# A two-layer decoder on one core: queries and keys of the causal attentions laid out by DMA through DRAM instead of by padded products, and a new rank for the order of work

## The chip, the cores and the metric

The kernel runs on one core of a Trainium2 chip. The metric is the device time of one execution in microseconds. Three runs of the kernel before gave 4504.14 (the median), 4497.92 and 4506.57 us.

## What is computed

Sixteen sequences of 512 rows and 256 features pass through two decoder layers. Each layer is a causal self-attention, a cross-attention to 64 context rows, and a feed-forward part, each added to its input and normalised. All data are 32-bit floats. Only the two causal attentions are touched by the change. Cut to what matters:

```python
# layer 0: 16 heads of 16 features, a bias that depends on (i - j)
q, k, v = split(x @ Wqkv.T)                       # heads() splits 256 into 16 x 16
logits = q @ k.T / 4 + fourier_bias(alpha, beta)[h, i - j]
x = layernorm(x + softmax(causal(logits)) @ v @ Wout.T)
x = layernorm(x + cross_attention_0(x, ctx))      # 16 heads
x = layernorm(x + experts(x))                     # 8 routed (top 2) and 2 shared
# layer 1: q, k, v through latents of 64 features, no bias
q, k, v = x @ wq_lat @ wq_heads, x @ wk_lat @ wk_heads, x @ wv_lat @ wv_heads
x = layernorm(x + softmax(causal(q @ k.T / 4)) @ v @ w_proj + b_proj)
x = layernorm(x + cross_attention_1(x, ctx))      # one head
x = layernorm(x + feed_forward(x))                # 1024 hidden, sine, relu
```

The bias of layer 0 is a sum of cosines and sines of (i - j). With the angle-sum formulas it becomes 16 more features beside the 16 of each head: fixed cosines and sines on the query side, the same mixed by alpha and beta on the key side.

## The kernel before

**Layout of an attention.** A group is four heads, and there are four groups. A tile q or k of a group is 128 x 512: head j has partitions 32 j to 32 j + 31, of which the first 16 hold its features and the other 16 the extra ones. Score products then contract over 32 partitions, and four heads run on four row bands of TensorE's array at once. In layer 1 the extra rows are zeros, but for row 16: there k holds -1 and q later receives the row's maximum, so that the product subtracts it.

**How q and k come about** (`queries_keys`, lines 825 and 869). The weight matrices are padded on the host (`_laid_out`): each head's 16 columns stand in 32, the others are zero. So every group needs products of its own with 128 output rows, half of them padding. In layer 0 a group takes two products of 512 columns for q, two for k and one more (`kmat` by `qfeat`) for k's bias features; VectorE evicts q and adds `qfeat`, ScalarE evicts k. In layer 1 a group takes one product of 64 contracted rows for q, and one on the array's other 64 rows for k; ScalarE evicts both, k with the bias `onerow`. The results are the tiles q and k themselves, with no transfer in between.

**The attention** (`causal_attention`, line 557). The scores are made twice: once with queries as rows (`max_unit`), reduced by VectorE to row maxima, and once with keys as rows (`exp_unit`), from which the maximum is subtracted within the product (layer 0: the product `mrow` by `minus16`; layer 1: by q's extra row) and which ScalarE exponentiates, GpSimd masks and a product with the values (`po`) consumes. Units of a group's maxima run beside units of the exponentials of the group before. q and k have three buffers each.

**The order of work.** The stages of a sequence are a0 (attention of layer 0), d0 (cross-attention 0 and experts), a1 and d1 (cross-attention 1 and feed-forward). `places` (line 1402) pairs a1 of one sequence with d0 of the next, and d1 with a0 of the one after. All operations are recorded first, each with an engine, an estimated cost and an estimated time until its result can be used. `run_plan` (line 346) then lists them: at each step it takes, among the operations that can start soonest, the one with the lowest rank. The rank is set in `stage` (line 318): the stage's place plus the share of the stage's TensorE cost that is recorded before the operation, less 0.5 for operations that use one of the pools named in `score_pools`. The instructions are issued in that order, and `Pinned` (line 330) keeps every engine's own order as planned. TensorE, VectorE, ScalarE and GpSimd are pinned so; DMAs on SyncE's queue (SP), x, context, mask and the output, are not. Every engine's queue is in order: a waiting instruction holds up all behind it on that engine.

**Buffers.** Pool `d4` (six of 4 KB per partition) serves the d stages: transposed input, queries, score tiles e, results. Pool `h` (three) serves the experts' hidden rows. Three PSUM banks `pd` take all products but scores and attention values.

Of the kernel before, what the change touches and what calls it, by code (L numbers as in the profile page):

```python
# [26 lines left out]
F32 = mybir.dt.float32  # L27
# [3 lines left out]
ALU = mybir.AluOpType  # L31
# [28 lines left out]
def decoder_kernel(ctx: ExitStack, tc: tile.TileContext, a: dict, out: bass.AP):  # L60
# [34 lines left out]

    wqk0 = weight("wqk0", 2 * NG * P)
    qfeat = const.tile([P, S], F32, tag="qfeat", name="qfeat")
    load(qfeat, a["qfeat"])
    kmat = const.tile([P, NG * P], F32, tag="kmat", name="kmat")
    load(kmat, a["kalpha"])  # L100
    with tc.tile_pool(name="once", bufs=1) as once:
        for name, op in (("kbeta", ALU.add), ("kbeta_n", ALU.subtract)):
            part = once.tile([P, NG * P], F32, tag="part", name=name)
            load(part, a[name])
            nc.vector.tensor_tensor(kmat, kmat, part, op)
    wv0 = weight("wv0", D)
    wout0 = weight("wout0", D)
# [21 lines left out]
    nc.gpsimd.memset(minus16, -1.0)  # L129
    onerow = const.tile([P, 1], F32, tag="onerow", name="onerow")  # L130
    load(onerow, a["onerow"])

# [35 lines left out]
    for n, name in enumerate(("wq_lat", "wk_lat", "wv_lat")):  # L168
        load(wlat[:, :, n], a[f"L1_attn_{name}"].rearrange("(c p) n -> p c n", p=P))
    wqk1 = const.tile([P, NG * P], F32, tag="wqk1", name="wqk1")  # L170
    load(wqk1, a["wqk1"])
# [93 lines left out]
    e_pool, os_pool = Pool("e", 4), Pool("os", 1)  # L265
    d4, h_pool, u_pool = Pool("d4", 6), Pool("h", 3), Pool("u", 1)
    ctx_pool, mi_pool, cT_pool, vbd_pool = Pool("ctx", 1), Pool("mi", 4), Pool("cT", 3), Pool("vbd", 2)
# [47 lines left out]

    score_pools = ("pa", "e", "q", "k", "os", "mrow", "m", "r", "a4")

    def stage(place, record, *args):

        stage_ops.clear()  # L320
        record(*args)
        done, total = 0.0, sum(o.cost for o in stage_ops if o.engine == "PE") or 1.0
        for o in stage_ops:

            ahead = 0.5 if any(s.pool.name in score_pools for s in o.slots) else 0.0
            o.rank = place + done / total - ahead
            if o.engine == "PE":
                done += o.cost
# [14 lines left out]

    pe, dve, act, pool = map(Pinned, (nc.tensor, nc.vector, nc.scalar, nc.gpsimd))

# [211 lines left out]
    def causal_attention(queries_keys, exact):  # L557
# [6 lines left out]
        def max_unit(g, w, pair):  # L564
# [33 lines left out]

            return first, None, masks, follow, [q, k], [two]

        def exp_unit(g, w, pair):
# [41 lines left out]

            return first, None if exact else second, None, follow, [q, k] + ([] if exact else [groups[g]["mrow"]]), [two]

# [15 lines left out]
        def rows_of_maxima(g):  # L661
            q, wide, token = groups[g]["q"], *((whole, "whole") if exact else (parts, "parts"))
            p = ps_d([P, 512], "pr", F32 if exact else BF16)

            def turn():
                for i in range(NT):
                    pe.transpose(
                        p.t[:, i * P : (i + 1) * P],
                        wide[:, i].rearrange("p j r -> p (j r)"),
                        ident if exact else ident16,  # L670
                    )

            PE(0.45 if exact else 0.25, turn, [token], [p])
            if exact:
                DVE(S, lambda: dve.tensor_tensor(q.t, p.t, q.t, ALU.add), [p, q], [q])
            else:
                mrow = groups[g]["mrow"] = mrow_pool([P, S], "mrow", BF16)
                ACT(S, lambda: act.copy(mrow.t, p.t), [p], [mrow])
# [64 lines left out]
        while last is None or n <= last:  # L743
# [5 lines left out]

            while len(groups) < NG and (n_m + 2) // 6 >= len(groups):  # L750
                g = len(groups)
                q, k = queries_keys(g)
                groups[g] = dict(q=q, k=k, m=small([P, NT, NG, 1], "m"))
            for g in [g for g, r in rows_at.items() if r == n]:
# [53 lines left out]
    def fill_values(t, p):  # L808

        ACT(D, lambda: act.copy(vp[:, t, :, :HD], p.t[:, :D].rearrange("p (h d) -> p h d", d=HD)), [p], [("vp", t)])  # L810

    def attention0(x):
        xT = features(x, a4)
# [10 lines left out]

        def queries_keys(g):
            q, k = q_pool([P, S], "q"), k_pool([P, S], "k")
            p = ps_d([P, 512], "pq")
            PE(
                mm_cost(S, 2),
                lambda: mm_chunks(p.t, lambda c: wqk0[:, c, g * P : (g + 1) * P], lambda c: xT.t[:, c]),  # L830
                both(xT), [p],
            )
            DVE(S, lambda: dve.scalar_tensor_tensor(q.t, p.t, HD**-0.5, qfeat, ALU.mult, ALU.add), [p], [q])
            p2 = ps_d([P, 512], "pk")

            def keys():
                for c in range(NC):
                    pe.matmul(
                        p2.t, wqk0[:, c, (NG + g) * P : (NG + g + 1) * P], xT.t[:, c], start=(c == 0), stop=False
                    )  # L840
                pe.matmul(p2.t, kmat[:, g * P : (g + 1) * P], qfeat, start=False, stop=True)

            PE(mm_cost(S, 3), keys, both(xT), [p2])
            ACT(S, lambda: act.copy(k.t, p2.t), [p2], [k])
            return q, k

        yT = causal_attention(queries_keys, False)
        project_norm(x, yT, wout0)

    def attention1(x):  # L850
# [17 lines left out]

        def queries_keys(g):
            q, k = q_pool([P, S], "q"), k_pool([P, S], "k")  # L870
            p, p2 = ps_d([P, 512], "pq"), ps_d([P, 512], "pk")
            cols = slice(g * P, (g + 1) * P)
            PE(
                mm_cost(S),
                lambda: pe.matmul(p.t, wqk1[0:64, cols], lat.t[0:64, 0], start=True, stop=True), [lat[0]], [p],
            )
            ACT(S, lambda: act.mul(q.t, p.t, HD**-0.5), [p], [q])
            PE(
                mm_cost(S),
                lambda: pe.matmul(p2.t, wqk1[64:128, cols], lat.t[64:128, 0], start=True, stop=True), [lat[0]], [p2],  # L880
            )
            ACT(S, lambda: act.activation(k.t, p2.t, AF.Identity, bias=onerow), [p2], [k])
            return q, k

        for t in range(NT):
# [8 lines left out]
            fill_values(t, pv)  # L894
        yT = causal_attention(queries_keys, True)
        project_norm(x, yT, wproj)
# [469 lines left out]
    def inputs(b):  # L1366
        x, c, mi = x_pool([P, NT, D], "x"), ctx_pool([SK, D], "ctx"), mi_pool([P, SK], "mi", I32)
        op(
            "SP", 0.1, lambda: nc.sync.dma_start(x.t, a["x"][b].rearrange("(t p) d -> p t d", p=P)),
            (), rows_of(x), wait=6.0,  # L1370
        )

        def small_ones():
            nc.sync.dma_start(c.t, a["ctx_1024"][b])
            nc.sync.dma_start(mi.t, a["mask_BxS2_ik0"][b].partition_broadcast(P))

        op("SP", 0.1, small_ones, (), [c, mi], wait=4.0)
        seqs[b] = [x, c, mi]
# [14 lines left out]
    def d1(b):  # L1393
# [3 lines left out]
        op(  # L1397
            "SP", 0.1, lambda: nc.sync.dma_start(out[b].rearrange("(t p) d -> p t d", p=P), x.t),
            rows_of(x), (), wait=5.0,
# [18 lines left out]
def _laid_out(i):  # L1418
# [6 lines left out]
    wqkv = np.asarray(i["L0_attn_Wqkv"]).T  # L1425
    qk = z((D, 2, H, 32), np.float32)
    qk[:, :, :, :HD] = wqkv[:, : 2 * D].reshape(D, 2, H, HD)
    a["wqk0"] = qk.reshape(D, -1)
    a["wv0"] = wqkv[:, 2 * D :]
    a["wout0"] = np.asarray(i["L0_attn_Wout"]).T  # L1430
    heads = z((2, 64, H, 32), np.float32)
    heads[0, :, :, :HD] = np.asarray(i["L1_attn_wq_heads"]).reshape(64, H, HD)
    heads[1, :, :, :HD] = np.asarray(i["L1_attn_wk_heads"]).reshape(64, H, HD)
    a["wqk1"] = heads.reshape(P, -1)

    R = HD // 2
    omega = 10000.0 ** (-2.0 * np.arange(R) / HD)
    angle = omega[:, None] * np.arange(S)[None, :]
    trig = z((4, 32, S), np.float32)
    trig[:, 16:24], trig[:, 24:32] = np.cos(angle), np.sin(angle)  # L1440
    a["qfeat"] = trig.reshape(P, S)
    alpha, beta = np.asarray(i["L0_attn_alpha"]), np.asarray(i["L0_attn_beta"])
    ka, kb, kn = (z((P, H, 32), np.float32) for _ in range(3))
    for r in range(R):
        cos, sin = 16 + r, 24 + r
        ka[cos, :, cos] = ka[sin, :, sin] = alpha[:, r]
        kb[cos, :, sin] = kn[sin, :, cos] = beta[:, r]
    a["kalpha"], a["kbeta"], a["kbeta_n"] = (k.reshape(P, -1) for k in (ka, kb, kn))
    p = np.arange(P)
    a["hmask"] = (p[:, None] // HD == np.arange(H // NC)[None, :]).astype(np.float32)  # L1450
    a["vmask"] = (p[:, None] // SK == np.arange(2 * HD)[None, :] // HD).astype(np.float32)
    a["onerow"] = -(p % 32 == HD).astype(np.float32)[:, None]
    a["prio"] = np.tile(np.arange(NE, 0, -1, dtype=np.float32), (P, 1))
# [18 lines left out]
```

## Time and profile before

| | us |
|---|---|
| median of three runs | 4504.14 |
| the profiled execution, its time | 4507.05 |
| its span, first to last instruction | 4505.3 |
| TensorE's matmuls, busy (PE) | 4260.3 |
| VectorE, busy (DVE) | 2641.7 |
| ScalarE, busy (ACT) | 1571.0 |
| GpSimd, busy (POOL) | 1205.5 |
| first instruction of TensorE, which waits for the first context | 50.0 |

In the profile PE is TensorE's matmuls and PEld its weight loads. A row of a timeline gives the start, the duration, the engine, the line of the code that issued it (all work of the plan has the line of one helper), the operation, out <- in by the program's names and a count of records; a bracket gives the idle time of the engine before it and what ended it. The profile counts two records for one product of 32-bit floats. Matmuls overlap, so the distance of two starts says more than a duration. A row of busy times by stretch gives the stretch, its length, the busy time of PE, PEld, DVE, ACT and POOL, the granted clock of TensorE (1.00 is full speed), the busy share of the DMA engines and GB/s. A row of a DMA issue ends with the size of one transfer and the median time from issue to landing.

### The profile page before, as it was taken

What the parts mean: (1) busy time and instruction counts of PE and PEld (TensorE: products, weight loads), DVE (VectorE), ACT (ScalarE), POOL (GpSimd) and SP (SyncE); (2) the same over time, 40 slices, a digit from 0 to 9 for tenths busy, and PEclk for the clock granted to TensorE, in tenths of its full rate; (3) what the DMA queues carried; (4) which work ended last, traced back from release to release, by engine and by line L of the source; (5) the groups of instructions that cost most, each with busy time, mean ns of one, the idle gap of its engine ahead of it and who ended that gap; (6) DMA issues with size and microseconds to landing.
All of it is one profiled execution on the core that took longest, in us unless ns stands there. A gap on an engine that the chain in (4) does not pass through costs nothing.

```text
span 4505.3 us, 65388 instructions
## 1 busy us (share of the span) xinstructions
PE 4260.3 (95%) x26816; PEld 2372.9 (53%) x26816; DVE 2641.7 (59%) x5317; ACT 1571.0 (35%) x2273; POOL 1205.5 (27%) x2221
## 2 busy tenths in 40 slices
PE   4999999999999999999999999999999999999897
PEld 2455555555555555555555555555555555555544
DVE  2456566565666556665565665656665565655554
ACT  1323242434314243242433414343242432424333
POOL 0313231323313133131322313233131332313322
PEclk8999999999999999999999999999999999999998
DMA  4000000000000000000000000000000000000000
GB/s 129 2 1 1 2 10 2 10 1 2 10 2 10 1 2 10 2 10 1 11 1 2 10 2 10 1 2 10 2 10 1 6 6 1 10 1 6 1 1 10
DMA packets 41355, 35.05 MB, mean 8 GB/s; under 512 B 11424, under 2 KB 39904, under 8 KB 41056
## 3 DMA queue, kind: packets, MB, share of 16 engines
q1 hardware_dynamic: 30736, 23.70, 1.7%
q10 hardware_dynamic: 10320, 7.17, 0.5%
q8 instruction: 211, 3.46, 0.3%
q14 instruction: 88, 0.72, 0.1%
HBM read 22.47 MB, written 8.39 MB: 7 GB/s over the span
## 4 chain that ended last, share of the span: by engine, by line
PE 84%; ACT 6%; DVE 5%; POOL 2%; issue 1%; DMA 1%; SPq 0%; ACTq 0%; POOLq 0%; DVEq 0%
PE pa L340 22%; PE pf L340 8%; PE pq L340 7%; PE pg L340 7%; PE pe L340 6%; PE pu L340 6%; PE po L340 6%; PE pp L340 5%; PE pk L340 4%; ACT e L340 4%; PE pt L340 4%; PE ps L340 3%; PE pv L340 3%; DVE m L340 2%; PE pl L340 1%
## 5 line engine op out<-in xcount | busy, mean ns | idle before, releaser
L340 DVE TENSOR_REDUCE m<-pa 128x2 f32<-128x1024 f32 (+3 forms) x1024 | 805.6, 818 | 425.7 <-PE pa L340 423.5
L340 ACT ACTIVATE e<-pa 128x1024 f32<-128x1024 f32 (+1 forms) x768 | 662.6, 884 | 685.9 <-PE pa L340 647.7
L340 PE MATMUL pa<-q,k 32*128 32x512 f32 (+3 forms) x4096 | 665.5, 472 | 23.0 <-ACT e L340 19.7
L340 POOL TENSOR_SCALAR_AFFINE_SELECT e<-e 128x256 f32<-128x256 f32 x1024 | 437.9, 441 | 918.1 <-ACT e L340 906.8
L340 PE MATMUL pa<-k,q 32*128 32x512 f32 (+3 forms) x4096 | 616.6, 471 | 51.3 <-DVE m L340 40.2
L340 PEld LDWEIGHTS pa<-k,q 32*128 32x128 f32 x4096 | 271.4, 185 | 345.3 <-issue 155.0
L340 PEld LDWEIGHTS pa<-q,k 32*128 32x128 f32 x4096 | 297.2, 186 | 170.5 <-ACT e L340 67.3
L340 PE MATMUL po<-e,vp 128*32 128x512 f32 (+3 forms) x4096 | 360.5, 447 | 18.0 <-POOL e L340 15.9
L340 ACT ACTIVATE h<-pg 128x512 f32<-128x512 f32 x160 | 95.5, 597 | 708.2 <-PE pg L340 708.2
L340 POOL TENSOR_TENSOR rs<-rs,minus_half 128x2 f32<-128x2 f32 x192 | 133.4, 716 | 708.3 <-DVE rs L340 707.6
L340 PE MATMUL pe<-w,h 128*128 128x256 f32 x1280 | 307.6, 381 | 0.8 <-DVE h L340 0.8
L340 PE MATMUL pg<-xT,w 128*128 128x512 f32 x640 | 303.9, 597 | 0.0
L340 PE MATMUL pu<-xT,w 128*128 128x512 f32 x640 | 301.8, 594 | 0.0
L340 PEld LDWEIGHTS pe<-w,h 128*128 128x128 f32 x1280 | 240.6, 190 | 97.2 <-issue 59.0
L340 PE MATMUL pf<-xT,L_ffn_W 128*128 128x512 f32 x512 | 248.3, 610 | 0.2 <-ACT xT L340 0.2
L340 POOL CAST parts<-m 128x16 bf16<-128x16 f32 x192 | 55.2, 288 | 711.4 <-DVE m L340 703.2
L340 DVE SCALAR_TENSOR_TENSOR x<-pe,r_pick,x 128x256 f32<-128x256 f32 x512 | 215.5, 477 | 42.8 <-PE pe L340 42.8
L340 PE MATMUL pf<-ff,act 128*128 128x256 f32 x1024 | 235.7, 384 | 3.9 <-ACT act L340 3.9
L340 DVE SCALAR_TENSOR_TENSOR h<-h,pg 128x512 f32<-128x512 f32 x160 | 110.0, 687 | 197.9 <-ACT h L340 197.9
L340 PEld LDWEIGHTS <-ident 128*128 128x128 bf16 x1536 | 92.5, 97 | 245.3 <-issue 217.3
L340 PE MATMUL pa<-cmask,ident 128*128 128x128 bf16 (+1 forms) x1536 | 220.1, 242 | 0.0
L340 PEld LDWEIGHTS pf<-ff,act 128*128 128x128 f32 x1024 | 193.2, 192 | 37.4 <-ACT act L340 6.2
(180 smaller groups left out, 6359.9 us busy)
## 6 DMA issues: line engine op xcount, KB each, us to landing
x<-in_x SPq DMA_DIRECT2D x16, 512.0 KB, 3.9
out_x<-x SPq DMA_DIRECT2D x16, 512.0 KB, 2.9
wqk<-in_wqk ACTq DMA_DIRECT2D x1, 1024.0 KB, 6.0
w<-in_L_ffn_routed_w SPq DMA_DIRECT2D x8, 128.0 KB, 3.8
w<-in_L_ffn_routed_w ACTq DMA_DIRECT2D x8, 128.0 KB, 4.0
w<-in_L_ffn_routed_w ACTq DMA_DIRECT2D x1, 1024.0 KB, 9.6
L_ffn_W<-in_L_ffn_W SPq DMA_DIRECT2D x1, 1024.0 KB, 8.0
ff<-in_L_ffn_W ACTq DMA_DIRECT2D x1, 1024.0 KB, 9.0
```

The source lines that it names most:

```text
L340: return tc.keep_in_program_order(f(*args, **kw))
```

## The change

**Products without padding.** `wqk0` has 512 columns instead of 1024 and `wqk1` 256 instead of 512: no padding, and within each half c of the 16 heads (8 heads) the columns are ordered by feature, then head. `products(c)` makes q and k of 8 heads at once: in layer 0 two products of 512 columns for each, in layer 1 one for each, both in one operation. ScalarE evicts all of them (q scaled) to tiles from the new pools `qh` and `kh`.

**Placing by DMA.** Eight tensors `way` in DRAM, [32 rows, 8 heads, 512], one for each layer, for q and k, and for each half. Their upper 16 rows are filled once at the start: cosines and sines for layer 0's q; the features mixed by alpha and beta for its k (one product of 16 contracted rows for each half, evicted and stored); zeros for layer 1's q; zeros and one row of -1 for its k. For each half the evicted q and k are written to the lower 16 rows, and each group's q and k tiles are read back with the head as the outer index. All of it is on SP's queue, which is now pinned to the plan too; x, context, mask and output stand on the same queue. Score units depend on the q and k tiles that are read.

**Ranks.** `stage` ranks by the mean of the PE share and of 1 less the longest remaining chain over the longest chain of the stage. Half a stage ahead are now all operations of a0 and a1, and none of d0 and d1. In `causal_attention` the next group's q and k are asked for two units earlier.

**Buffers.** `d4` has five instead of six, `h` two instead of three. `qfeat` (as an SBUF tile), `onerow` and the wide `kmat` go.

```diff
+    dram = ctx.enter_context(tc.tile_pool(name="dram", bufs=1, space=bass.MemoryType.DRAM))
+    way = [
+        [[dram.tile([32, 8, S], F32, tag=f"way{l}{n}{c}", name="way") for c in range(NC)] for n in range(2)]
+        for l in range(2)
+    ]
+    for l, n, name in ((0, 0, "trig8"), (1, 0, "zeros8"), (1, 1, "minus8")):
+        for c in range(NC):
+            load(way[l][n][c][HD:], a[name])
...
+        for c in range(NC):
+            mixed = once_ps.tile([P, S], F32, tag="mixed", name="mixed")
+            nc.tensor.matmul(mixed, kmat[:, c * P : (c + 1) * P], trig, start=True, stop=True)
+            kfeat = once.tile([P, S], F32, tag=f"kfeat{c}", name="kfeat")
+            nc.vector.tensor_copy(kfeat, mixed)
+            load(way[0][1][c][HD:].rearrange("r h s -> (r h) s"), kfeat)
...
-    d4, h_pool, u_pool = Pool("d4", 6), Pool("h", 3), Pool("u", 1)
+    d4, h_pool, u_pool = Pool("d4", 5), Pool("h", 2), Pool("u", 1)
+    qk_pools = Pool("qh", 2), Pool("kh", 2)
...
+        tail, inside = {}, {o.index for o in stage_ops}
+        for o in reversed(stage_ops):
+            tail[o.index] = o.cost + o.wait + max((tail[n] for n in o.after if n in inside), default=0.0)
+        longest = max(tail.values())
...
+        ahead = 0.5 if record in (a0, a1) else 0.0
         for o in stage_ops:
-            ahead = 0.5 if any(s.pool.name in score_pools for s in o.slots) else 0.0
-            o.rank = place + done / total - ahead
+            o.rank = place + (done / total + 1.0 - tail[o.index] / longest) / 2 - ahead
...
-            while len(groups) < NG and (n_m + 2) // 6 >= len(groups):
+            while len(groups) < NG and (n_m + 4) // 6 >= len(groups):
...
+    def spread_heads(products, layer):
+        def queries_keys(g):
+            c, tiles = g // 2, (q_pool([P, S], "q"), k_pool([P, S], "k"))
+            if g % 2 == 0:
+                for n, t in enumerate(products(c)):
+                    op(
+                        "SP", 0.6,
+                        lambda n=n, t=t: sp.dma_start(
+                            way[layer][n][c][:HD].rearrange("r h s -> (r h) s"), t.t
+                        ),
+                        [t], [("way", layer, n, c)], wait=2.4,
+                    )
+            for n, t in enumerate(tiles):
+                heads = slice(g % 2 * NG, g % 2 * NG + NG)
+                op(
+                    "SP", 0.6,
+                    lambda n=n, t=t: sp.dma_start(t.t, way[layer][n][c].rearrange("r h s -> h r s")[heads]),
+                    [("way", layer, n, c)], [t], wait=2.8,
+                )
+            return *tiles, list(tiles)
+        return queries_keys
...
+        def products(c):
+            both_of = []
+            for n in range(2):
+                p, t = ps_d([P, 512], "pqk"), qk_pools[n]([P, S], "qk")
+                cols = slice(n * D + c * P, n * D + (c + 1) * P)
+                PE(
+                    mm_cost(S, 2),
+                    lambda p=p, cols=cols: mm_chunks(p.t, lambda c: wqk0[:, c, cols], lambda c: xT.t[:, c]),
+                    both(xT), [p],
+                )
...
+            def product():
+                pe.matmul(p.t, wqk1[0:64, cols], lat.t[0:64, 0], start=True, stop=True)
+                pe.matmul(p2.t, wqk1[64:128, cols], lat.t[64:128, 0], start=True, stop=True)
```

More of the change, by code (lines that the diff above doesn't have):

```diff
@@ L93, in decoder_kernel @@
     make_identity(nc, ident)
[L96 to L101, printed above, removed]
+    wqk0 = weight("wqk0", 2 * D)
+    dram = ctx.enter_context(tc.tile_pool(name="dram", bufs=1, space=bass.MemoryType.DRAM))
[6 more added lines that the diff above has]
+            load(way[l][n][c][HD:], a[name])
+    with tc.tile_pool(name="once", bufs=1) as once, tc.tile_pool(
+        name="once_ps", bufs=1, space=bass.MemoryType.PSUM
+    ) as once_ps:
+        trig = once.tile([HD, S], F32, tag="trig", name="trig")
+        load(trig, a["trig8"][:, 0])
+        kmat = once.tile([HD, D], F32, tag="kmat", name="kmat")
+        load(kmat, a["kalpha"])
         for name, op in (("kbeta", ALU.add), ("kbeta_n", ALU.subtract)):
-            part = once.tile([P, NG * P], F32, tag="part", name=name)
+            part = once.tile([HD, D], F32, tag=name, name=name)
             load(part, a[name])
             nc.vector.tensor_tensor(kmat, kmat, part, op)
+        for c in range(NC):
[4 more added lines that the diff above has]
+            load(way[0][1][c][HD:].rearrange("r h s -> (r h) s"), kfeat)
     wv0 = weight("wv0", D)
@@ L129, in decoder_kernel @@
     nc.gpsimd.memset(minus16, -1.0)
-    onerow = const.tile([P, 1], F32, tag="onerow", name="onerow")
-    load(onerow, a["onerow"])
     wq_x0 = weight("L0_xattn_wq_w", D)
@@ L169, in decoder_kernel @@
         load(wlat[:, :, n], a[f"L1_attn_{name}"].rearrange("(c p) n -> p c n", p=P))
-    wqk1 = const.tile([P, NG * P], F32, tag="wqk1", name="wqk1")
+    wqk1 = const.tile([P, D], F32, tag="wqk1", name="wqk1")
     load(wqk1, a["wqk1"])
@@ L314, in op @@
         return o
-    score_pools = ("pa", "e", "q", "k", "os", "mrow", "m", "r", "a4")
     def stage(place, record, *args):
@@ L342, in __getattr__ @@
             return call
-    pe, dve, act, pool = map(Pinned, (nc.tensor, nc.vector, nc.scalar, nc.gpsimd))
+    pe, dve, act, pool, sp = map(Pinned, (nc.tensor, nc.vector, nc.scalar, nc.gpsimd, nc.sync))
     def run_plan():
@@ L597, in follow @@
                 )
-            return first, None, masks, follow, [q, k], [two]
+            return first, None, masks, follow, groups[g]["ready"], [two]
         def exp_unit(g, w, pair):
@@ L642, in follow @@
                 op("POOL", 0.43 * len(blocks), causal, [e], [e])
-            return first, None if exact else second, None, follow, [q, k] + ([] if exact else [groups[g]["mrow"]]), [two]
+            return first, None if exact else second, None, follow, groups[g]["ready"] + ([] if exact else [groups[g]["mrow"]]), [two]
         def spread(g):
@@ L674, in rows_of_maxima @@
             if exact:
-                DVE(S, lambda: dve.tensor_tensor(q.t, p.t, q.t, ALU.add), [p, q], [q])
+                own = [q]
+                DVE(S, lambda: dve.tensor_tensor(q.t, p.t, q.t, ALU.add), [p, *own], own)
             else:
@@ L748, in causal_attention @@
             count_m, count_e = (1, 1) if can_m and can_e else (2 * can_m, 2 * can_e)
-            while len(groups) < NG and (n_m + 2) // 6 >= len(groups):
+            while len(groups) < NG and (n_m + 4) // 6 >= len(groups):
                 g = len(groups)
-                q, k = queries_keys(g)
-                groups[g] = dict(q=q, k=k, m=small([P, NT, NG, 1], "m"))
+                q, k, ready = queries_keys(g)
+                groups[g] = dict(q=q, k=k, ready=ready, m=small([P, NT, NG, 1], "m"))
             for g in [g for g, r in rows_at.items() if r == n]:
@@ L823, in attention0 @@
             fill_values(t, p)
[L825 to L847, printed above, removed]
+        def products(c):
[8 more added lines that the diff above has]
+                )
+                if n == 0:
+                    ACT(S, lambda p=p, t=t: act.mul(t.t, p.t, HD**-0.5), [p], [t])
+                else:
+                    ACT(S, lambda p=p, t=t: act.copy(t.t, p.t), [p], [t])
+                both_of.append(t)
+            return both_of
+        yT = causal_attention(spread_heads(products, 0), False)
         project_norm(x, yT, wout0)
@@ L867, in attention1, with products @@
         DVE(S, lambda: dve.tensor_copy(lat.t[:64, 1], p2.t[:64]), [p2], [lat[1]])
-        def queries_keys(g):
-            q, k = q_pool([P, S], "q"), k_pool([P, S], "k")
+        def products(c):
+            cols = slice(c * P, (c + 1) * P)
             p, p2 = ps_d([P, 512], "pq"), ps_d([P, 512], "pk")
[L872 to L876, printed above, removed]
-            ACT(S, lambda: act.mul(q.t, p.t, HD**-0.5), [p], [q])
[L878 to L882, printed above, removed]
+            q, k = (p([P, S], "qk") for p in qk_pools)
+            def product():
+                pe.matmul(p.t, wqk1[0:64, cols], lat.t[0:64, 0], start=True, stop=True)
+                pe.matmul(p2.t, wqk1[64:128, cols], lat.t[64:128, 0], start=True, stop=True)
+            PE(mm_cost(S), product, [lat[0]], [p, p2])
+            ACT(S, lambda: act.mul(q.t, p.t, HD**-0.5), [p], [q])
+            ACT(S, lambda: act.copy(k.t, p2.t), [p2], [k])
             return q, k
@@ L894, in attention1 @@
             fill_values(t, pv)
-        yT = causal_attention(queries_keys, True)
+        yT = causal_attention(spread_heads(products, 1), True)
         project_norm(x, yT, wproj)
@@ L1368, in inputs @@
         op(
-            "SP", 0.1, lambda: nc.sync.dma_start(x.t, a["x"][b].rearrange("(t p) d -> p t d", p=P)),
+            "SP", 0.1, lambda: sp.dma_start(x.t, a["x"][b].rearrange("(t p) d -> p t d", p=P)),
             (), rows_of(x), wait=6.0,
@@ L1373, in small_ones @@
         def small_ones():
-            nc.sync.dma_start(c.t, a["ctx_1024"][b])
-            nc.sync.dma_start(mi.t, a["mask_BxS2_ik0"][b].partition_broadcast(P))
+            sp.dma_start(c.t, a["ctx_1024"][b])
+            sp.dma_start(mi.t, a["mask_BxS2_ik0"][b].partition_broadcast(P))
         op("SP", 0.1, small_ones, (), [c, mi], wait=4.0)
@@ L1397, in d1 @@
         op(
-            "SP", 0.1, lambda: nc.sync.dma_start(out[b].rearrange("(t p) d -> p t d", p=P), x.t),
+            "SP", 0.1, lambda: sp.dma_start(out[b].rearrange("(t p) d -> p t d", p=P), x.t),
             rows_of(x), (), wait=5.0,
@@ L1425, in _laid_out, with by_rows @@
     wqkv = np.asarray(i["L0_attn_Wqkv"]).T
-    qk = z((D, 2, H, 32), np.float32)
-    qk[:, :, :, :HD] = wqkv[:, : 2 * D].reshape(D, 2, H, HD)
-    a["wqk0"] = qk.reshape(D, -1)
+    def by_rows(w):
+        return w.reshape(len(w), NC, 8, HD).transpose(0, 1, 3, 2).reshape(len(w), D)
+    a["wqk0"] = np.concatenate([by_rows(wqkv[:, :D]), by_rows(wqkv[:, D : 2 * D])], 1)
     a["wv0"] = wqkv[:, 2 * D :]
     a["wout0"] = np.asarray(i["L0_attn_Wout"]).T
[L1431 to L1434, printed above, removed]
+    a["wqk1"] = np.concatenate([by_rows(np.asarray(i[f"L1_attn_w{n}_heads"])) for n in "qk"])
     R = HD // 2
@@ L1438, in _laid_out @@
     angle = omega[:, None] * np.arange(S)[None, :]
-    trig = z((4, 32, S), np.float32)
-    trig[:, 16:24], trig[:, 24:32] = np.cos(angle), np.sin(angle)
-    a["qfeat"] = trig.reshape(P, S)
+    trig = np.concatenate([np.cos(angle), np.sin(angle)]).astype(np.float32)
+    a["trig8"] = np.repeat(trig[:, None], 8, 1)
     alpha, beta = np.asarray(i["L0_attn_alpha"]), np.asarray(i["L0_attn_beta"])
-    ka, kb, kn = (z((P, H, 32), np.float32) for _ in range(3))
+    ka, kb, kn = (z((HD, H, HD), np.float32) for _ in range(3))
     for r in range(R):
-        cos, sin = 16 + r, 24 + r
+        cos, sin = r, R + r
         ka[cos, :, cos] = ka[sin, :, sin] = alpha[:, r]
         kb[cos, :, sin] = kn[sin, :, cos] = beta[:, r]
-    a["kalpha"], a["kbeta"], a["kbeta_n"] = (k.reshape(P, -1) for k in (ka, kb, kn))
+    a["kalpha"], a["kbeta"], a["kbeta_n"] = (by_rows(k.reshape(HD, -1)) for k in (ka, kb, kn))
+    a["zeros8"], a["minus8"] = z((2, HD, 8, S), np.float32)
+    a["minus8"][0] = -1.0
     p = np.arange(P)
@@ L1451, in _laid_out @@
     a["vmask"] = (p[:, None] // SK == np.arange(2 * HD)[None, :] // HD).astype(np.float32)
-    a["onerow"] = -(p % 32 == HD).astype(np.float32)[:, None]
     a["prio"] = np.tile(np.arange(NE, 0, -1, dtype=np.float32), (P, 1))
```

## The prediction

> **What bounds the kernel now.** I read the page first (busy times, clock row, chain), then the busy times of one period, then TensorE's timeline where queries and keys are made, then the DMA rows.
>
> ```profile
> span 4505.3 us, 65388 instructions
> PE 4260.3 (95%) x26816; PEld 2372.9 (53%) x26816; DVE 2641.7 (59%) x5317; ACT 1571.0 (35%) x2273; POOL 1205.5 (27%) x2221
> ...
> PE 84%; ACT 6%; DVE 5%; POOL 2%; issue 1%; DMA 1%; SPq 0%; ACTq 0%; POOLq 0%; DVEq 0%
> ```
>
> TensorE is busy 95% of the span and carries 84% of the chain that ended last; no other engine passes 59%. Two recurring timeline starts are one sequence apart (2025.60 and 2297.40): a period is 271.8 us. Its row, and four rows around the longest late gap, are (time, then busy us by engine, then granted clock):
>
> ```profile
> 2025.60:2297.40 271.80, 262.83 (x1678) 146.68 (x1678) 164.65 (x332) 98.13 (x142) 75.25 (x138) 1.00 0.02 5
> 4235.00:4240.00 5.00, 0.00 (x0) 0.00 (x0) 4.09 (x19) 0.00 (x0) 1.61 (x3) 0.61 0.00 0
> 4240.00:4245.00 5.00, 4.08 (x19) 3.75 (x19) 2.49 (x7) 1.17 (x2) 1.56 (x4) 0.50 0.01 3
> 4245.00:4250.00 5.00, 5.00 (x18) 3.97 (x18) 2.20 (x10) 0.00 (x0) 2.06 (x4) 0.50 0.00 0
> 4250.00:4255.00 5.00, 5.00 (x9) 1.98 (x9) 2.25 (x12) 1.38 (x3) 0.00 (x0) 0.68 0.00 0
> ```
>
> In a period TensorE is idle 9.0 us and the clock is full: what leaves TensorE shortens the kernel, and a wait put on TensorE lengthens it one for one. The later rows show that a gap costs more than itself: TensorE stood still for 7.13 us until 4240.92, and the clock stayed at half until about 4253.2 (0.68 of 5 us is 3.2 us at half), 12.3 us into the work that followed.
>
> **What the change takes off TensorE.** The timeline of the first attention's start, and of the second's:
>
> ```profile
> 2059.71 1.88 PE L340 MATMUL pq<-xT,wqk 128*128 128x512 f32 x4
> 2061.42 1.88 PE L340 MATMUL pk<-xT,wqk 128*128 128x512 f32 x4
> 2063.14 1.02 PE L340 MATMUL pk<-qfeat,kmat 128*128 128x512 f32 x2
> 2064.00 1.88 PE L340 MATMUL pq<-xT,wqk 128*128 128x512 f32 x4
> ```
> ```profile
> 2237.54 0.69 PE L340 MATMUL pq<-lat,wqk 64*128 64x512 f32 x1
> 2237.55 0.69 PE L340 MATMUL pk<-lat,wqk 64*128 64x512 f32 x1
> ...
> 2238.64 2.42 PE L340 MATMUL pv<-wv,lat 64*128 64x256 f32 x8
> ```
>
> Read the starts, not the durations. A product of 512 columns is two records: 0.86 us (four in 1.72). The first attention makes 20 such products per sequence (four groups: two for q, two for k, one for kmat), 320 in all; the changed program has 128 in their place, 8 per sequence. 12 x 0.86 x 16 = 165.1 us. In the second attention q and k lie on different rows of the array and run together: 1.10 us for the pair above, the four groups of that period 1.10, 0.97, 1.90 (apart) and 1.06, sum 5.03. Two pairs remain, 2.12. Saved 2.91 x 16 = 46.6. Together 211.7 us, 13.2 per sequence: the gain if nothing waits.
>
> Evictions: 64 q evictions leave VectorE (0.692 us each) and ScalarE makes them at 0.597; in the second attention ScalarE makes 64 instead of 128. Neither bounds; cover is TensorE's own stream. I take zero.
>
> **What it adds.** Per attention, 4 writes and 8 reads of 256 KB on SP's queue, which carried 3 to 4 transfers a sequence before. SP issues in order, so a read behind a write waits for that write's landing, and everything behind waits too. Bytes are no problem (6.3 MB per 270 us; 242 GB/s was moved in 2244 to 2246). The latency is, because TensorE's order is fixed: all its work waits behind the first score product. The rows nearest:
>
> ```profile
> x<-in_x SPq DMA_DIRECT2D x16, 512.0 KB, 3.9
> out_x<-x SPq DMA_DIRECT2D x16, 512.0 KB, 2.9
> ...
> qfeat<-in_qfeat SPq DMA_DIRECT2D x1, 256.0 KB, 3.3
> ```
>
> A packet of 2,048 bytes took 84 ns at the median in the trace's DMA records, one of 1,024 took 46. Over sixteen engines 256 KB is 8 packets each, 0.7 us. The out row less half its data (1.47 to 0.7) gives a write 2.2 us; a read is 2.4 + 0.7 = 3.1, near qfeat's 3.3.
>
> [...] The writes go out as 128 rows. The reads as built have 128 rows on the SBUF side but 4 heads x 32 rows on the DRAM side[...]. All loads before have 64 or 128 rows, so no row shows this shape. By the row a read is 3.1 us[...].
>
> First attention, from the end of the q product of the first half (T = 0): evicted at 0.8, write issued at 1.0, landed 3.2. Reads of q for groups 0 and 1 are issued at 3.3 and 3.7; k's write lands at 4.9 and its reads follow. Data start about 5.2, and in SP's order q0 (2.7), q1 (2.7), a write of the second half (0.7) and k0 (2.7) end at 14.0, k0 landed 14.5. TensorE has until its first score product: three more products 5.16, four value products 3.44 (16 records in 3.45), eight transposes 0.88: 9.5. Wait 5.0 us; with sixteen engines k0 lands near 9 and the wait is nil.
>
> Second attention: write 1.0 to 3.2, k's 1.6 to 3.8, then only q0 and k0 ahead: 5.2 + 5.4 + 0.5 = 11.1. Work to the first score: 16 down products at 0.431 (6.9) and a latent product (1.72): 8.6. Wait 2.4. Group 3 there reads into a buffer that frees late: landing 8.1 after, work between 6.9; of the 1.2 I count 0.8, since up to 0.5 of idle is there now. The other groups have 14 us or more in TensorE's order, except group 3 of the first attention (9.7 against 8.1): zero; their cover is experts and cross-attention.
>
> The clock. [...] The row above says 6.1 for one gap; gaps of 1.64 and 1.31 us near 4311 were followed by 6.8 us at half. I take 2.6[...] for the 5.0 us wait, 0.9 for the 2.4 us one.
>
> Start and end: the first attention has no cover. First scores came 11.5 us after 57.9, where value products began; now products come first and k0 lands near 74.3 instead of 69.4 (+4.9); its group 3 waits about 4.4; the last attention has 5.9 us of work instead of 8.6 (+2.7). Sum 12.0. Setup loads move similar bytes: zero, at most 3 either way.
>
> New ranks and one buffer fewer in d4 and h: the order of instructions shows the expert pattern unchanged (each h is read before its buffer is due again); cross-attention 0 has two score tiles in flight instead of three, covered by the other attention. Idle is 9.0 us a period; I take zero, and 2 us a sequence either way, 32 us.
>
> Sum: -211.7 + 16 x (5.0 + 2.6 + 2.4 + 0.9 + 0.8) + 12.0 = -12.5. The profiled execution took 4507.05, so 4494.5; it lies 2.9 above the median of the runs, 4504.14. Forecast 4492.
>
> **The rivals.**
> *Reads land in time* (all engines share them, or the cover is longer): -211.7 + 12 and some of the 2 us per sequence: about 4310. For: the rows of every load before; against: the shape on the DRAM side. 0.14.
> *The clock stays at half as after 4240.9* (slower): place, first score product of each attention; behind it stands router work of 8-column products, as in that gap. Price 6.1 instead of 2.6 and 1.7 instead of 0.9: 4.3 x 16 = 69, giving 4561. It decides from 0.8 us per sequence above my sum. 0.28.
> *Not doing what it says*: the second attention's products already ran in pairs, so if all four had, only 2 x 1.06 x 16 = 34 goes, 13 less: still case one.
>
> **How the numbers follow.** The likeliest, four engines with my sum, 0.58: 4492, own range 4450 to 4535 (32 for order, 0.6 us a sequence for the landing). Its shares: faster 0.32, same 0.10, slower 0.16. Reads in time: faster 0.14. Half clock: slower 0.24, same 0.02, faster 0.02. A measurement of this kernel tells 0.2% (9 us) from no change. Range 4395 to 4570: it leaves out most of the reads-in-time case (0.12) and the upper end of the half-clock case (0.08).
>
> **What would show it.** Products of 512 columns in the first attention 128, TensorE busy less by about 210. Reads of the way tiles landing after 5 us or more, k later than q; a wait of TensorE's pa on a DMA of 3 to 6 us at each first attention, about 2 at each second, half clock behind them. Reads landing in 3.1 us, or no pa row waiting for DMA, would make me wrong towards 4310; other idle growing (h, e, DVE m) would say the ranks matter.

## The result and the profile after

Four runs of the changed kernel gave 4467.83 us in the median (4460.96 to 4472.18), four of the kernel before 4501.74. The ratio is 0.9923, with a 95% interval of 0.9904 to 0.9941: 34 us faster. The forecast was 4492 with a range of 4395 to 4570. The profiled execution took 4460.96 us; its page:

```profile
span 4459.2 us, 65399 instructions
PE 4094.1 (92%) x26308; PEld 2290.5 (51%) x26308; DVE 2605.6 (58%) x5255; ACT 1506.1 (34%) x2181; POOL 1185.9 (27%) x2221
...
PE 72%; DMA 9%; DVE 5%; ACT 4%; POOL 1%; issue 1%; SPq 0%; POOLq 0%; DVEq 0%; ACTq 0%
```

TensorE lost 166 us of busy time, and its part of the chain fell from 84 to 72%. DMA, 1% before, is now 9% of the chain. The waits of TensorE (what waited on what, us in total, how often, the longest):

```profile
PE pa L362 <- DMA k<-way: 123.7, 47, 5.2
PE pa L362 <- DVE m L362: 50.2, 46, 2.0
PE pt L362 <- DVE x L362: 42.0, 21, 7.3
```

The first row did not exist before. The other two were:

```profile
PE pa L340 <- DVE m L340: 43.3, 92, 1.5
PE pt L340 <- DVE x L340: 22.8, 9, 7.1
```

The start of a first attention, the stretch that the prediction stepped through, on TensorE and on SP's queue:

```profile
2057.93 7.03 PE L362 MATMUL pqk<-xT,wqk 128*128 128x512 f32 x16
2064.79 2.75 PE L362 MATMUL pv<-wv,xT 128*128 128x256 f32 x12
2067.38 1.04 PE L362 MATMUL pt<-ident,x 128*128 128x128 f32 x8
2068.26 1.03 PE L362 MATMUL pv<-wv,xT 128*128 128x256 f32 x4
2074.11 2.09 PE L362 MATMUL pa<-k,q 32*128 32x512 f32 x8 [4.82 <-DMA k<-way]
```
```profile
2060.47 2.04 SPq L362 DMA_DIRECT2D way<-qk  x2
2062.68 1.16 SPq L362 DMA_DIRECT2D q<-way  x2
2063.90 0.45 SPq L362 DMA_DIRECT2D way<-qk  x1
2064.45 1.28 SPq L362 DMA_DIRECT2D k<-way  x2
```

The first q product ends 1.72 us after 2057.93, at 2059.65. The read of q follows its write by 2.2 us (SP waited for such writes 68 times, 193.8 us in all), k's reads are issued from 2064.45, and the score product stops waiting at 2074.11: 9.7 us after the first of k's reads is issued and 14.5 after the q product. TensorE's own work, all of it in the first four rows, was over 4.8 us sooner. The stretches below show a period and the start of a second attention:

```profile
2069.29:2335.50 266.21, 250.84 (x1638) 140.53 (x1639) 161.62 (x326) 93.37 (x136) 73.75 (x138) 0.97 0.08 28
2225.00:2230.00 5.00, 3.32 (x18) 1.16 (x17) 0.92 (x2) 0.00 (x0) 0.00 (x0) 1.00 0.26 102
...
2245.00:2250.00 5.00, 3.56 (x19) 2.41 (x20) 3.66 (x9) 0.00 (x0) 1.75 (x3) 0.77 0.04 16
2250.00:2255.00 5.00, 3.63 (x17) 2.01 (x16) 4.88 (x10) 0.59 (x1) 1.75 (x4) 0.50 0.00 0
2255.00:2260.00 5.00, 5.00 (x20) 1.47 (x14) 0.69 (x1) 2.99 (x3) 1.72 (x3) 0.70 0.61 160
```

TensorE is busy 12.0 us less in a period, but idle 15.4 instead of 9.0 us. While reads alone run (second row) the DMA engines are busy to 0.26, about four of sixteen, and move 102 GB/s, with four reads issued from 2220.49 to 2222.29 and no other until 2236.69. In the last three rows the clock is at half for about 10 us where no DMA is waited for: that was not in the prediction.

**Where the time went.** I compared the two traces by the distance of TensorE's starts: a distance less its idle part is work, half of the work time at half clock is counted as lost (eight records of `pt` took 1.04 us at 2067.38, at full clock, and 2.21 at 2251.85, at half), and the rest is work at full clock. The removed products took 215.4 us (forecast 211.7); the first attentions have 256 records of `pqk`, 128 products. The score products, which are the same, took 80 us less at full clock (15 us less before the half clock is taken out). Idle time rose by 119 us (leaving out 39 us before the first real work, which count as idle only because of the small product `mixed` at 11 us), and half clock in work from 96 to 319 us, a loss of 112. The half clock and the 80 us needed runs.

### The profile page after: what moved, and what is told of

The parts are those of the page before. It is cut to its first block, busy times and chain, and to the rows that moved or that the text cites. A ratio compares the mean times of both kernels' runs of the same rounds, so it can differ in the third digit from the quotient of the medians.

```text
span 4459.2 us, 65399 instructions
## 1 busy us (share of the span) xinstructions
PE 4094.1 (92%) x26308; PEld 2290.5 (51%) x26308; DVE 2605.6 (58%) x5255; ACT 1506.1 (34%) x2181; POOL 1185.9 (27%) x2221
## 4 chain that ended last, share of the span: by engine, by line
PE 72%; DMA 9%; DVE 5%; ACT 4%; POOL 1%; issue 1%; SPq 0%; POOLq 0%; DVEq 0%; ACTq 0%
PE pa L362 21%; DMA k<-way 8%; PE pg L362 7%; PE pf L362 7%; PE po L362 6%; PE pe L362 6%; PE pu L362 6%; PE pq L362 5%; PE pp L362 4%; PE pt L362 3%; PE ps L362 2%; ACT e L362 2%; PE pqk L362 2%; DVE m L362 1%; PE pv L362 1%
## 5 line engine op out<-in xcount | busy, mean ns | idle before, releaser
L362 PE MATMUL pa<-k,q 32*128 32x512 f32 (+3 forms) x4096 | 663.2, 503 | 193.6 <-DMA k<-way 123.7
L362 POOL TENSOR_SCALAR_AFFINE_SELECT e<-e 128x256 f32<-128x256 f32 x1024 | 416.0, 420 | 964.4 <-ACT e L362 957.2
L362 PE MATMUL pa<-q,k 32*128 32x512 f32 (+3 forms) x4096 | 637.3, 480 | 5.2 <-DVE m L362 3.2
L362 PEld LDWEIGHTS pa<-k,q 32*128 32x128 f32 x4096 | 296.2, 195 | 494.7 <-issue 328.2
L362 PEld LDWEIGHTS pa<-q,k 32*128 32x128 f32 x4096 | 274.1, 188 | 123.9 <-issue 41.6
L362 PE MATMUL pg<-xT,w 128*128 128x512 f32 x640 | 317.8, 620 | 0.0
L362 PE MATMUL pa<-cmask,ident 128*128 128x128 bf16 (+1 forms) x1536 | 231.5, 253 | 0.0
```

What stands on the lines that cost most here:

```text
L362: return tc.keep_in_program_order(f(*args, **kw))
```

## The experiments

Theory A: the reads run on four engines and TensorE stands for that. Theory R: the new ranks gave the unforeseen 80 us. Against them: other causes of the wait, ranks worth nothing, or ranks that do harm.

**Reads on sixteen engines.** Only the shape of the tensors in DRAM changes; the writes and the loads at the start follow it.

```diff
-        [[dram.tile([32, 8, S], F32, tag=f"way{l}{n}{c}", name="way") for c in range(NC)] for n in range(2)]
+        [[dram.tile([8, 32, S], F32, tag=f"way{l}{n}{c}", name="way") for c in range(NC)] for n in range(2)]
...
-                    lambda n=n, t=t: sp.dma_start(t.t, way[layer][n][c].rearrange("r h s -> h r s")[heads]),
+                    lambda n=n, t=t: sp.dma_start(t.t, way[layer][n][c][heads].rearrange("h r s -> (h r) s")),
```

> The changed kernel with one thing altered: the tensors in DRAM are stored as 8 heads x 32 rows instead of 32 rows x 8 heads, so that a read of four heads is 128 rows in a row (outermost 128 on both sides), while a write becomes 16 x 8 rows on the DRAM side. The order of every engine is that of the changed kernel. Theory A (the reads run on four DMA engines because their outermost count is 4, keys land 9.5 us after their issue, and TensorE stands for it, 123.7 us in all, with half clock behind it): reads land in about 3 to 4 us, the share of the DMA engines during reads goes from 0.26 to 0.6 or more, TensorE's wait for the DMA of k falls below 20 us, and the time falls by about 100 us (the wait alone) to 160 us (with its part of the clock): 4310 to 4370. Rival B (the time to land is set by the write and the queue, not by the number of engines): the wait stays above 90 us and the time within 20 us of 4468. Rival C (half clock comes from the planned order around VectorE, not from the DMA wait): the wait goes, but half clock stays above 250 us of the span, and the gain is 100 us or a little less.

Measured: 4307.56 us, ratio 0.9565 (0.9552 to 0.9578), 160 us under the changed kernel. Landing times in the DMA rows (for the changed kernel the page gave none), a stretch of reads, the same score product, and what is left of waits:

```profile
way<-qk SPq DMA_DIRECT2D x128, 256.0 KB, 2.9
q<-way SPq DMA_DIRECT2D x128, 256.0 KB, 2.8
k<-way SPq DMA_DIRECT2D x128, 256.0 KB, 2.9
```
```profile
2137.00:2140.00 3.00, 3.00 (x14) 2.12 (x13) 1.85 (x3) 2.42 (x4) 0.00 (x0) 1.00 0.93 292
```
```profile
1990.83 1.03 PE L362 MATMUL pv<-wv,xT 128*128 128x256 f32 x4
1991.96 1.14 PE L362 MATMUL pa<-k,q 32*128 32x512 f32 x8
```
```profile
PE pa L362 <- DVE m L362: 58.0, 60, 2.2
PE pt L362 <- DVE x L362: 41.8, 21, 7.3
...
PE pa L362 <- DMA k<-way: 7.0, 11, 1.1
```

In the same order of work, reads land in 2.9 us, all engines share them (0.93 at 292 GB/s), the score product follows the last value product without a wait, and the wait on k falls from 123.7 to 7.0 us. A holds (the time lies 2 us under its range). Rival C holds in part: half clock is still 261 us (367 in the changed kernel). Of the 152 us between the two profiled spans, 111 are idle time and 47 half clock, less 7 of work that grew.

**Ranks and buffers, one at a time.** The ranks of before in the changed kernel; the new ranks in the kernel before; the buffers taken from the kernel before.

```diff
-        ahead = 0.5 if record in (a0, a1) else 0.0
...
-            o.rank = place + (done / total + 1.0 - tail[o.index] / longest) / 2 - ahead
+            ahead = 0.5 if any(s.pool.name in score_pools for s in o.slots) else 0.0
+            o.rank = place + done / total - ahead
```

> The changed kernel with the rank rule of before (share of PE recorded before, less half a stage for operations of the score pools, the two new pools among them); DMA placing and buffers as changed. Theory R (the new ranks gave the 80 us by which score products took less time than in the kernel before, work that I had not foreseen): the time rises by 40 to 80 us over the changed kernel, to 4510 to 4550, and the score products' time goes back up. Rival (the score products got shorter because fewer products stand among them, whatever the rank): within 20 us of 4468. Second rival (the new ranks cost, by the waits on VectorE that grew from 66 to 92 us and the half clock at the start of layer 1's attention): the time falls by 20 to 60 us, to 4410 to 4450, with fewer than 30 spells of half clock instead of 49.

Measured: 4638.37 us, ratio 1.0295 (1.0273 to 1.0317), beyond all three expectations: without the new ranks the placing would have made the kernel slower. The direction is R's; the size, 170 us, is twice what R said.

> The kernel before with the new rank rule alone. Theory R (the new ranks shorten the score products by 80 us of work in which they stand beside others): faster by 30 to 80 us, 4420 to 4470. Rival (ranks worth nothing by themselves, as I predicted, 0 with 32 us either way): within 32 us of 4502. Second rival (the new ranks bring waits on VectorE and half clock): slower by 20 to 100 us, with more half clock than the 111 us of before.

 The edit is the one above the other way round.

Measured: 4454.07 us, ratio 0.9888 (0.9873 to 0.9902): 49 us faster by ranks alone. R's range holds, and "worth nothing" falls. R's mechanism holds only in part: idle time went down by 48 us, work at full clock by 22 (the score products alone by 37, not 80), and half clock took back 17.

```diff
-    d4, h_pool, u_pool = Pool("d4", 6), Pool("h", 3), Pool("u", 1)
+    d4, h_pool, u_pool = Pool("d4", 5), Pool("h", 2), Pool("u", 1)
```

> The kernel before with five instead of six buffers in pool d4 and two instead of three in pool h, nothing else. I predicted zero for it with at most 2 us a sequence: within 32 us of 4502, and likely within 10. Rival (the lost buffers hold up the experts and cross-attention 0, and a part of the new waits of TensorE comes from them): slower by over 32 us, with waits of TensorE for the release of h or of d4's tiles that the kernel before doesn't have.

Measured: 4507.54 us, ratio 1.0011 (1.0003 to 1.0019): 5 us slower, far inside the 32 us. The term of zero holds.

**The old ranks with short reads.** The edit of the ranks, on the sixteen-engine version.

> Reads on sixteen engines with the rank rule of before. Known: new ranks gain 49 us in the kernel before, and 170 in the changed one (4638 without them). Theory R1 (they gain more there because they put time between the reads' issue and the first score product): with short reads the gain shrinks to about the 50 of before, 4340 to 4370. Theory R2 (the gain lies in how the score products follow each other, in whatever way the keys come): it stays near 170, 4460 to 4490.

Measured: 4476.29 us, ratio 0.9938 (0.9923 to 0.9952). R1 falls, R2 holds: the ranks are worth 169 us with short reads as with long ones (170). They do not hide the reads. In the two profiled executions the old ranks have 63 us more idle time, 29 more lost to half clock and 94 more of work at full clock (that of the old ranks took 4494 us, 18 over its median). The score products account for all of the 94. The waits of TensorE that head the list with the old ranks:

```profile
PE pa L360 <- DVE m L360: 106.1, 135, 2.5
```

With the new ranks that was 58.0 us in 60 waits. So 48 of the 63 us of idle time lie where VectorE's reductions of the maxima hold up the next scores. That VectorE also stands behind the 94 us is likely, but not shown.

**Which half of the rank rule.** On sixteen engines: only the half stage ahead for whole attentions, or only the mean with the longest chain.

```diff
-            o.rank = place + (done / total + 1.0 - tail[o.index] / longest) / 2 - ahead
+            o.rank = place + done / total - ahead
```

> Reads on sixteen engines; of the new rank rule only the half stage by which all operations of the two attentions are ahead; the longest chain is left out, and the share of PE counts whole. Between the new ranks (4308) and the old (4476) lie 169 us. Theory R-ahead (it matters that the products, values and reads of an attention move up together with its scores, which the old rule left behind in d's place): 4300 to 4350. Rival R-chain (the chain part orders VectorE's and ScalarE's steps, and so shortens the score products): 4430 to 4480. In between: each does a part.

Measured: 4336.91 us, ratio 0.9626 (0.9612 to 0.9641).

```diff
-        ahead = 0.5 if record in (a0, a1) else 0.0
...
+            ahead = 0.5 if any(s.pool.name in score_pools for s in o.slots) else 0.0
```

> Reads on sixteen engines; of the new rank rule only the mean with the longest chain; ahead by half a stage are again the operations of the score pools, the two new pools among them. Theory R-ahead: near the old ranks, 4430 to 4480. Rival R-chain: near the new ones, 4300 to 4350.

Measured: 4435.85 us, ratio 0.9849 (0.9835 to 0.9864). Moving whole attentions ahead is worth 139 of the 169 us alone, the chain 40 alone; R-ahead holds. Which of the moved operations matters is open.

**One layer at a time.** In the sixteen-engine version one layer's queries and keys come again from padded products (`queries_keys` of the kernel before, returning its tiles as `ready`).

```diff
-        yT = causal_attention(spread_heads(products, 1), True)
+        yT = causal_attention(queries_keys, True)
```

> Reads on sixteen engines and placing by DMA in layer 0 alone; layer 1 makes q and k by padded products as before. Theory G (layer 1's removed products had covered VectorE's reductions of the maxima; in each sequence TensorE now stands 2.01 us there, and about 11 us of half clock follow: 14 x (2.0 + 5.6) = 107 us against the 47 us that the products took): the gap of 2.01 us goes, half clock falls from 261 to about 120 us, and the time falls by about 60, to 4230 to 4270. Rival (the gap comes from the new order, not from the missing products): it stays, and the products come on top, 4340 to 4370.

Measured: 4336.44 us, ratio 0.9638 (0.962 to 0.9655), 29 us slower than with both layers placed (24 to 45 by its single runs). Theory G's mechanism is there: no gap of 2.01 us, half clock 155 instead of 261 us. But its balance was wrong. Work at full clock rose by 85 us, of which q and k products are 50 and score products 33; that outweighs the clock.

```diff
-        yT = causal_attention(spread_heads(products, 0), False)
+        yT = causal_attention(queries_keys, False)
```

> Reads on sixteen engines and placing by DMA in layer 1 alone; layer 0 makes q and k by padded products as before; ranks and buffers as changed. Beside it stands the kernel before with the new ranks, 4454. Theory G (the products taken off layer 1 cost more than they took): 4480 to 4520, with the gap of 2.01 us before the same score product and half clock behind it. Rival (the saved products count): about 4454 - 47 = 4407, and no such gap.

Measured: 4433.29 us, ratio 0.9845 (0.9833 to 0.9858), 21 us faster than the new ranks on the kernel before. Neither expectation's number: the gap and its half clock (221 us) are there, as G said, and still the products are worth more. Both runs agree: layer 1 gives 21 to 29 us of the 47 its products took.

The gap itself, on TensorE in the kernel before, then in the sixteen-engine version, and there on VectorE:

```profile
2242.06 0.40 PE L340 MATMUL pa<-cmask,ident 128*128 128x128 bf16 x4
...
2243.35 1.02 PE L340 MATMUL pq<-lat,wqk 64*128 64x512 f32 x2
2244.19 1.12 PE L340 MATMUL pk<-lat,wqk 64*128 64x512 f32 x2
2245.25 1.16 PE L340 MATMUL pa<-k,q 32*128 32x384 f32 x16
```
```profile
2156.61 0.40 PE L362 MATMUL pa<-cmask,ident 128*128 128x128 bf16 x4
2156.84 0.61 PE L362 MATMUL pr<-ident,whole 128*128 128x128 f32 x4
2159.45 3.06 PE L362 MATMUL pa<-k,q 32*128 32x384 f32 x16 [2.01 <-DVE m L362]
...
2164.84 2.21 PE L362 MATMUL pt<-ident,x 128*128 128x128 f32 x8 [1.36 <-DVE x L362]
```
```profile
2156.95 0.40 DVE L362 BATCH_NORM_STATS2 st<-x 128x6 f32<-128x256 f32 x1
...
2157.49 0.69 DVE L362 TENSOR_TENSOR q<-pr,q 128x512 f32<-128x512 f32 x1
2158.10 2.34 DVE L362 TENSOR_REDUCE m<-pa 128x2 f32<-128x1024 f32 x2
```

Before, q and k products of later groups stood between two units of scores. Now a short transpose stands there, and the next unit waits for a bank that VectorE reduces only after five statistics of the other sequence and the sum into q. In each of fourteen sequences TensorE stands for 2.01 us, soon after it stands again for 1.4 to 1.8 us (last row on TensorE), and half clock follows; in the changed kernel's trace, where the same two waits stand in fourteen sequences, it lasts 6.8 to 13.7 us. With layer 0 alone placed, the planner puts value products and transposes behind that short transpose, and the only wait of the stretch, one unit sooner, is 1.31 us (first row below). With the new ranks but no placing, no wait for m is longer than 1.5 us (second row):

```profile
2162.13 1.72 PE L364 MATMUL pa<-k,q 32*128 32x512 f32 x8 [1.31 <-DVE m L364]
```
```profile
PE pa L343 <- DVE m L343: 30.1, 58, 1.5
```

So the new ranks alone do not make the gap. It comes with the removed products of layer 1, through the order that the planner finds without them.

**Telling the planner.** Four engines as changed, a longer time told for a read; then the same on sixteen engines.

```diff
-                    [("way", layer, n, c)], [t], wait=2.8,
+                    [("way", layer, n, c)], [t], wait=9.5,
```

> The changed kernel, its reads on four engines as they are, but the planner told that a read takes 9.5 us until it can be used instead of 2.8. Theory D (the wait is there because the order doesn't know of it, and there is work that could stand between): TensorE's wait for the DMA of k falls from 124 to below 60 us and the time to 4380 to 4440. Rival (nothing is left to put in between, or what is moved up costs as much elsewhere): within 25 us of 4468, with the idle time under other names.

Measured: 4435.54 us, ratio 0.9851 (0.9838 to 0.9863), 32 us faster than the changed kernel. The wait on k goes from 123.7 to 1.4 us:

```profile
PE pa L362 <- DMA k<-way: 1.4, 1, 1.4
```

What stands behind a waiting product in TensorE's order waits with it (4.82 us up to 2074.11 in the changed kernel); in another order the same reads cost TensorE almost no wait. Theory D holds, yet only a fifth of the 160 us that the four engines cost comes back.

> Reads on sixteen engines, in the order that is planned for reads of 9.5 us: the order of the run in which only the planner was told (4436), now with short reads. Theory (that order already hides the four-engine reads, and what it costs over the 4308 of the short order is other waits): within 20 us of 4436. Rival (four engines still cost where nothing can cover them, at the start, at the end and in reads that share the same four engines): 4380 or less.

Measured: 4418.93 us, ratio 0.9815 (0.9793 to 0.9837), inside the theory's 20 us. In this order four engines cost 17 us; the order itself costs 111 over the short one, and its first waits are 51.4 us on ScalarE's e and 45.8 on VectorE's x. Hiding the long reads saved 143 us (160 less 17) and cost 111.

**Buffers given back.** The edit of the buffers reversed, on the sixteen-engine version.

> Reads on sixteen engines (4308) with the buffers of before given back: six in pool d4 and three in pool h. My term for the buffers was zero, and in the kernel before their loss cost 5 us. If that holds under the new order too: within 10 us of 4308. Rival (cross-attention and experts, now behind the attentions, need the buffers more than they did): faster by 15 us or more, with shorter waits in those stages; it would then be the fastest version.

Measured: 4311.58 us, ratio 0.9577 (0.9564 to 0.9591). Zero, again. The fastest version stays the sixteen-engine one, 4307.56.

## Why the prediction came out as it did

The runs split the change into steps of medians (the buffers, 5 us or less, are left out):

| step | runs | predicted | measured |
|---|---|---|---|
| new ranks | 4502.6 to 4454.1 | 0 | -48.6 |
| products replaced by placing, short reads | 4454.1 to 4307.6 | -211.7 | -146.5 |
| reads on four engines | 4307.6 to 4467.8 | +199.2 (16 x 11.7 + 12.0) | +160.3 |
| sum | | -12.5 | -34.8 |

The split depends on the order of the steps. With the old ranks, placing with short reads gives only 26 us (4502.6 to 4476.3), and the ranks then give 169: most of what the products are worth is had only together with the new order. The step of the products also holds two small parts of the change that no run separates: the next group's q and k are asked for two units earlier, and SP's queue is pinned.

- *Products.* Right as TensorE's own time: 215.4 us against 211.7.
- *Reads on four engines.* Right in mechanism and place, and 39 us too dear. That four engines carry a read, 32 packets of 84 ns and so 2.7 us on each, was the author's assumption, against the rows of all earlier loads; no trace of the kernel before showed it. The busy share of 0.26, with four reads issued within 1.8 us of one another, and the 0.93 of the sixteen-engine run agree with it. The score product behind k0 started 14.5 us after the q product, where k0 was forecast to land. The waits came to 4.7 us a sequence where 5.0 was forecast, 1.8 for 2.4 (11.1 less 8.6 is 2.5) and 1.1 for 0.8; in all 123.7 us for 131. Half clock in work cost 47 us (319 less 225, halved) for 56.
- *Ranks.* "Idle is 9.0 us a period; I take zero, and 2 us a sequence either way" failed. They give 49 us in the kernel before and 170 in the changed one. Little idle time was taken for little to gain. But the order alone took 48 us off the idle time, about 3.0 a sequence, and part of the gain is not idle time at all: 22 us alone, and 94 with the placing, lie between the starts of products, where the profile counts TensorE as busy.
- *What the removed products hid.* This has no term in the prediction, though it took TensorE's stream as the cover of everything else. The profiled spans of the second step differ by 146 us: work at full clock fell by 249 (222 of it the products, 36 score products), idle time rose by 57 (waits for m by 28, for x by 21, for k by 7) and half clock cost 47. So 104 us came back as waits, all but 7 us of them on VectorE, and as their clock. Of the waits 48 us are the two in each of fourteen sequences at the start of layer 1's attention.
- *Clock.* The 2.6 and 0.9 us for the two waits were the author's estimates, not shown by a trace. Their sum, 3.5 us a sequence, was near the 3.0 that the waits on k cost. But of the 224 us by which half clock in work rose, 129 stay with short reads, most of them behind the wait for m. The second rival, 6.1 us behind each first wait, did not happen: 3.4 to 6.8 us of half clock, 1.7 to 3.4 lost, followed the first waits of 4.6 to 5.2 us.
- *Reads in time*, the first rival, is the sixteen-engine run: 4308 for about 4310 (which kept the 12.0 of start and end). The agreement is partly luck, since the ranks' 49 us and the 65 that the placing fell short nearly cancel.
- *Start and end.* Whether 12.0 was right as a sum stays open. The first score came 9.4 us later than before (forecast 4.9), but 4.5 of that stood ahead of the attention's first product (62.40 against 57.91), since the first context came 5.4 us later; the last attention waited 2.8 us, where 5.1 (2.4 and 2.7) was forecast. The second attention of the first sequence started 18 us later than before; short reads took back 19.

So 4468 lies within the 4450 to 4535 of the case held likeliest, and that case's mechanism, four engines, is the one that ran. The closeness is partly luck: three misses, -49 (ranks), +65 (what the removed products hid) and -39 (reads), add up to -22.

## What to carry to other kernels

Work that leaves the busiest engine may also have been the cover of another engine's work: before counting it as gain, look at what the next instruction waits for where it stood. When a tensor in DRAM is one's own, try its layout for the frequent transfer: here an outermost count of 128 instead of 4 on the DRAM side of the reads took the busy share of the DMA engines from 0.26 to 0.93, and that alone was worth 160 us, nearly five times the whole change. A better order of work also gains time that the profile counts as busy, and its gain can depend on the rest of the change (49 us alone, 170 with it), so a new rank is to be run by itself and with the rest.

## What was not expected of the hardware

In the changed kernel's trace half clock set in behind a gap of only 2.01 us and lasted 6.8 to 13.7 us, while waits of 4.6 to 5.2 us in dense work brought 3.4 to 6.8. Three stretches of the sixteen-engine version (the gap is in the first):

```profile
2155.00:2160.00 5.00, 2.99 (x23) 1.58 (x23) 4.83 (x13) 0.89 (x3) 0.17 (x1) 1.00 0.08 32
2160.00:2165.00 5.00, 3.63 (x21) 2.09 (x17) 3.59 (x12) 0.00 (x0) 1.99 (x3) 0.58 0.00 0
2165.00:2170.00 5.00, 5.00 (x19) 2.46 (x19) 3.51 (x8) 1.42 (x2) 2.82 (x4) 0.50 0.31 105
```

By the second row it began about 1.3 us behind the gap (0.58 of 5 us is 4.2 us at half). In eleven of fourteen sequences of the changed kernel it began 0.0 to 1.6 us behind the 2.01 us, in the other three only behind a second gap, of 1.82 us. Idle time alone does not decide when it sets in: behind a gap of 2.62 us, up to 364.57 in the same trace, the clock stayed full for 9.3 us, and at 271.4 half clock set in with no idle time of TensorE in the 3.4 us before.

What precedes its end is clearer. The traces of the kernel before and of the changed kernel hold 63 whole spells of half clock, of 3.4 to 30.7 us. In the last 3.4 us of each TensorE stood still for 0.31 us at most. But TensorE was also busy without a pause from 2165 to 2170 in the last row above, all of it at a clock of 0.50, and what kept it at half there no run here separates.
